# 256 KB copies of Wx into DRAM that nothing reads, issued from ScalarE's queue in the later steps of a recurrent layer

## The chip, the cores and the metric

The kernel runs on one core of a Trainium2 chip. The core has five engines with a queue of instructions each: TensorE (PE in the profile, its weight loads PEld), VectorE (DVE), ScalarE (ACT), GpSimd (POOL) and SyncE (SP), which issues transfers. Sixteen DMA engines move data between DRAM, where inputs and outputs lie, and the memory on the core. The metric is device time in microseconds (us) of one execution; lower is better.

## The reference

64 sequences of 256 steps with 1024 features pass through two layers, each added to its own input.

```python
# layer 0: x = x + rnn(x, h0 = cond)
xW = einsum('ntd,dh->nth', x, Wx) + b
def step(prev_h, xw):
    next_h = tanh(prev_h @ Wh + xw)
    return next_h, next_h
# layer 1: x = x + L1(x, q_pool = cond)
h = silu(q_pool @ W1.T + b1)
gate = sigmoid(h @ W2.T + b2)
# a Haar transform along time, every coefficient times gate, the inverse transform:
return v + a
```

Since every coefficient of the transform is multiplied by the same gate of its feature, the second layer comes down to a product: the output is (2 + gate) times the output of layer 0. The kernel keeps 2 + gate in the tile `factor`. All data are fp32.

## The kernel before

The recurrence is serial: step t needs the h of step t - 1. One step is the product of h (64 x 1024) with Wh (1024 x 1024), done by Strassen's scheme as seven products of half size (`strassen_product`, PE L199, 7 products of 16 fp32 matmuls of the program per step), with the sums between them on DVE and the copies out of PSUM and the tanh on ACT. The products x Wx do not depend on h. They are made for two steps at a time (128 rows, one "slab" of x) as three rounded partial products, 48 matmuls of 128x512 each (`x_matmul`, L278), to reach fp32 precision.

After twelve opening steps (`ALONE = 12`) the main loop, from step 12 on, works in groups of two steps. A group is: the x products of one coming slab (`beside_x`, "the x phase"), and then the h products of two steps ("the h phase"). The orders of PE, DVE, ACT, POOL and SP are written out by hand (`manual_schedule`): each engine runs its instructions in the order of the program text, and semaphores hold it where it needs the result of another.

The transfers of a group, all on SP's queue, in order: the finished sums of a slab go to DRAM (`store`, L390, 512 KB), a new slab of x is loaded (L121, 512 KB), the sums come back in the layout that a step needs (`reload`, L403, eight loads of 64 KB into `xw`), and a finished slab goes to the output (`store_y`, L634, 512 KB). The store of the sums has an added dependency (`not_ahead_of`) on `mark`, the copy of `u` in the group's second step, with the reason given in the code: "transfers stay out of the products of h". The relay, from that store until the `xw` of a step is back, must be done before `put_part` (L618) copies `xw` into the PSUM banks in which the step's products accumulate.

On ACT a step of the main loop is, in order: `y` (L778, the first product's copy out of PSUM), the cast of x for the coming slab (first step of a group only, L313), tanh of quarter 0 (L760), `put_part` for the next step's quarter 0 (first step only), `u` (L798), `put_part` 2 (first step only), tanh of quarters 3 and 2, tanh of quarter 1, `put_part` 1 (first step only). In the x phase ACT copies the two mixed sums out of PSUM (`take_mixed`, L323) and then does all three `put_part` of the next step. Each quarter of tanh is transposed by DVE (L764), and the transposed quarters and sums of them (`strassen_sides`, L229 to L232) are the weights of the next step's products. Their order there is: quarter 0, quarter 3, quarter 1, and then the sums.

Each DMA adds to one of eight completion semaphores, which are taken in turn over SP's and ACT's transfers together. A DMA is not issued before the semaphore's previous user has landed; where the issuing engine has not waited for that already, it waits at the DMA.

The first five slabs, which were finished before `factor` was known, are parked in DRAM and brought back step by step, one step in every second group (`kept_step`), all of it before step 80.

Of the kernel before, what the change touches and what calls it, by code (L numbers as in the profile page):

```python
# [53 lines left out]
F32 = mybir.dt.float32  # L54
# [6 lines left out]
N, T, D = 64, 256, 1024  # L61
P = 128
R = 32
Q = P // R
B = D // P
G = N // R
F = D // Q
W = G * F
# [3 lines left out]
M = 2  # L72
# [9 lines left out]
RINGS = 1024  # L82
BLOCK = 256
PLACE = 60


@with_exitstack
def tile_cond_resid(
# [14 lines left out]
    nc = tc.nc  # L103
# [7 lines left out]
    dram = ctx.enter_context(tc.tile_pool(name="dram", bufs=2, space=bass.MemoryType.DRAM))  # L111
# [82 lines left out]
    def strassen_product(out, a, i: int, first: bool = False) -> None:  # L194


        for k in range(KB):
            for q in range(Q):
                nc.tensor.matmul(  # L199
                    out=out[q * R : (q + 1) * R],  # L200
                    lhsT=a[:, k * R : (k + 1) * R],
                    rhs=wh_s.sides[i][k][:, q],
                    start=first and k == 0,
                    stop=k == KB - 1,
                    skip_group_check=True,
                    tile_position=(0, q * R),
                )
# [65 lines left out]
    def bank(tag: str, name: str):  # L273
        return one_pool.tile([P, HALF], F32, tag=tag, name=name)

    def x_matmul(acc, v, which: int, h: int, k: int, start=False, stop=False) -> None:

        nc.tensor.matmul(  # L278
            out=acc[h],
            lhsT=v[:, k * P : (k + 1) * P],  # L280
            rhs=wx_s[k][which][:, h * HALF : (h + 1) * HALF],
            start=start and k == 0,
            stop=stop and k == B - 1,
        )

    class XWork:
# [48 lines left out]
        def whole(self, aligned: bool = False) -> None:  # L335
# [8 lines left out]
            for h in range(2):  # L344
                for k in range(B):
                    if aligned and h == 1 and k == B - 2:
                        nc.tensor.addr_align(BLOCK, PLACE)
                    x_matmul(self.main, self.x0, 0, h, k, stop=True)
# [162 lines left out]
    kept, again, factor = [], [], None  # L511
# [103 lines left out]
    def put_part(t: int, j: int):  # L615

        part = bank(("acc", "m57", "gate")[j], f"acc{t}_{j}")[:, :E]
        nc.scalar.copy(part, xws[t // S][t % S][:, j])  # L618
        return part

    def residual(t: int, hT) -> None:
        v = x_step(t)
        nc.vector.tensor_add(v, v, blocks(hT))

    def not_ahead_of(dma, ins) -> None:
        tc.add_manual_dep(
            dma.ins,
            ins.ins.name,
            mybir.DependencyInfo(mybir.DependencyClass.Sync, mybir.DependencyReason.DATA),
            reason="transfers stay out of the products of h",  # L630
        )
# [26 lines left out]
    def beside_x(t: int, later, coming, scaled: list, end: int, mark):  # L658


        if later:
            d, dma = later.store()
            not_ahead_of(dma, mark)
        fresh = loaded[0] < NP
        load_next()
        if later:
            xws[later.i] = later.reload(d, True)
        now, half = coming, len(scaled) // 2
        many = now.i + 1 < NP and now.i <= end // S
        now.whole(not many)  # L670
        residual(t, hT)
        for r in scaled[: half + 1]:
            scale(pairs[r // S], r % S)
        if many:
            store_done(scaled[half])
            load_next()
        now.take_mixed()
        if mark:
            accs[:] = [put_part(t + 1, j) for j in range(3)]

        def prepare():
            if now.i + 1 == NP:
                return None
            nxt = XWork(now.i + 1)
            nxt.difference()
            nxt.low()
            return nxt

        nxt = prepare()
        if not fresh and not factors:  # L690

            x_n, factor_n = ends[0][:, :W], ends[0][:, W:]
            nc.vector.transpose(factor_n, factor)
            nc.vector.tensor_mul(x_n, x_n, factor_n)
            factors.append(factor_n)
        now.finish_half(0)
        now.finish_half(1)
        for r in scaled[half + 1 :]:
            scale(pairs[r // S], r % S)
        kept_step()  # L700
        if now.i <= end // S:
            d, _ = now.store()
            store_done(t)
            xws[now.i] = now.reload(d, True)
            if many:
                now = nxt
                now.cast()
                now.whole()
                now.take_mixed()
                nxt = prepare()  # L710
                now.finish_half(0)
                now.finish_half(1)
                return now, nxt
            return None, nxt
        store_done(t)
        return now, nxt

    again = []

    def kept_step() -> None:  # L720

# [25 lines left out]
    for t in range(ALONE, T):  # L747
        i, s = divmod(t, S)
        final = t == T - 1
        last_of_group = t == first + groups[0] - 1  # L750
        xw = xws[i][s]
        m16, m5, m7 = (bank(tag, f"{tag}_h{t}")[:, :E] for tag in ("m16", "main0", "main1"))
        y = sums.tile([P, 4, E], F32, tag="y", name=f"y{t}")
        u = sums.tile([P, E], F32, tag="u", name=f"u{t}")
        h = work.tile([P, W], F32, tag="h", bufs=1, name=f"h{t}")
        hT = None if final else work.tile([P, W], F32, tag="hT", name=f"hT{t}")
        nxt = [None] * 3

        def tanh(j: int) -> None:
            nc.scalar.activation(quad(h, j), quad(h, j), AF.Tanh)  # L760

        def transpose(j: int) -> None:
            if not final:
                nc.vector.transpose(quad(hT, j), quad(h, j))  # L764

        def put_next(j: int) -> None:
            if not last_of_group:
                nxt[j] = put_part(t + 1, j)

        def times_factor(v: slice) -> None:  # L770
            nc.vector.tensor_mul(h[:, v], h[:, v], ends[0][:, W + v.start : W + v.stop])

        def plus_x(v: slice) -> None:
            nc.vector.tensor_add(h[:, v], h[:, v], ends[0][:, v])
            nc.sync.dma_start(out=yT[i][:, W + v.start : W + v.stop], in_=h[:, v])

        strassen_product(m16, sides[1], 1, True)
        nc.scalar.copy(y[:, 0], m16)  # L778
        if t == first and coming is not None:
            coming.cast()  # L780
        strassen_product(accs[2], sides[4], 4)
        strassen_product(accs[0], sides[2], 2)
        strassen_product(m5, sides[5], 5, True)
        nc.vector.tensor_add(quad(h, 0), accs[0], y[:, 0])  # L784
        tanh(0)
        nc.vector.tensor_add(y[:, 3], m5, xw[:, 3])
        transpose(0)
        if final:
            times_factor(slice(0, E))
            plus_x(slice(0, E))  # L790
        elif t > T - 4:

            v = x_step(t - 1)
            nc.vector.tensor_mul(v, v, blocks(factor))
            store_y(i - 1) if t == T - S else None
        put_next(0)
        strassen_product(m16, sides[6], 6)
        mark = nc.scalar.copy(u, m16)  # L798
        nc.vector.tensor_add(y[:, 3], y[:, 3], u)
        nc.vector.tensor_add(y[:, 2], accs[2], u)  # L800
        put_next(2)
        strassen_product(m7, sides[7], 7, True)
        for o in (3, 2):
            nc.vector.tensor_add(quad(h, o), m7, y[:, o])
        tanh(3)
        tanh(2)
        nc.vector.tensor_add(y[:, 1], m5, u)
        transpose(3)
        strassen_product(accs[1], sides[3], 3)
        nc.vector.tensor_add(quad(h, 1), accs[1], y[:, 1])  # L810
        tanh(1)
        if final:
            times_factor(slice(F, W))
            times_factor(slice(E, F))
            plus_x(slice(E, F))
            plus_x(slice(F, W))
            break
        transpose(2)
        put_next(1)
        transpose(1)  # L820
        sides = strassen_sides(hT, t)
        accs = nxt
        if t == T - 2:

            last = slab("last")
            residual(t, hT)
            nc.vector.tensor_mul(blocks(last[:, :W]), x_step(t), blocks(factor))
            nc.sync.dma_start(out=yT[i][:, :W], in_=last[:, :W])
        elif last_of_group:
            group = range(first, t + 1)  # L830
            first = t + 1
            del groups[0]
            later, coming = beside_x(t, later, coming, list(group), t + groups[0], mark)
        else:
            residual(t, hT)
# [34 lines left out]
```

## Time and profile before

| what | value |
|---|---|
| median of 3 runs | 3045.01 us (3044.51 to 3046.28) |
| the profiled execution | 3044.8 us, of which the span from first to last instruction is 3043.0 us |
| granted TensorE clock | 1.000 |
| PE / PEld / DVE / ACT / POOL busy | 3033.8 / 2706.8 / 1797.0 / 871.0 / 844.4 us |
| time that DMA packets took, share of 16 engines' span | 27.5% (transfers), 1.1% (queue 8, instructions) |
| HBM read and written | 154.93 MB and 136.31 MB |
| one group of two steps | 23.47 us |

The group's length is read from the timeline: the x phases of two groups begin at 1143.87 and 1167.34 us. "Idle before" in the profile is time of the engine ahead of an instruction, with what ended it; "issue" is idle time in which the engine waited for nothing that the profile shows. Packets' shares are of the time of all 16 DMA engines. A view with a window cuts the window into 40 equal slices, each digit being the busy share in tenths.

### The profile page before, as it was taken

To read this page: it belongs to the slowest core of one execution; us is meant where nothing else is said; L and a number is where in the kernel's file an instruction comes from. 1 tells how busy PE (TensorE), PEld (TensorE's weight loads), DVE (VectorE), ACT (ScalarE), POOL (GpSimd) and SP (SyncE) were. 2 spreads that over 40 slices of the span, in tenths; PEclk is the share of its full clock that TensorE was granted. 3 is DMA by queue.
4 is the path that set the end of the run, shared out by engine and by line. 5 is a ranking of instruction groups with operands and counts; after the bars stand their busy time and mean duration, and the time that the engine had idled before them with its cause. 6 is when DMAs were issued, how large, how long until landed. Compare 5 with 4: busy or idle time off the path is not lost.

```text
span 3043.0 us, 144709 instructions
## 1 busy us (share of the span) xinstructions
PE 3033.8 (100%) x63862; PEld 2706.8 (89%) x63862; DVE 1797.0 (59%) x4928; ACT 871.0 (29%) x2641; POOL 844.4 (28%) x521
## 2 busy tenths in 40 slices
PE   9999999999999999999999999999999999999999
PEld 6888899889988898889888998899889988998888
DVE  8556555655555555555555565555655565565555
ACT  3222222222222222222222322232222222222222
POOL 2233333332223222322232223222222222222321
PEclk9999999999999999999999999999999999999999
DMA  7323323332222222222222222222222222222222
GB/s 264 123 90 115 101 100 100 109 107 86 86 101 98 86 86 99 100 86 86 96 99 89 86 93 97 95 86 89 102 95 86 86 102 97 86 86 102 97 86 76
DMA packets 164616, 300.59 MB, mean 99 GB/s; under 512 B 44192, under 2 KB 110496, under 8 KB 164000
## 3 DMA queue, kind: packets, MB, share of 16 engines
q1 hardware_dynamic: 163856, 290.81, 27.5%
q8 instruction: 514, 8.42, 1.1%
q14 instruction: 102, 0.84, 0.1%
q10 hardware_dynamic: 144, 0.52, 0.0%
HBM read 154.93 MB, written 136.31 MB: 96 GB/s over the span
## 4 chain that ended last, share of the span: by engine, by line
PE 98%; DMA 1%; POOL 0%; issue 0%; DVE 0%; SPq 0%; DVEq 0%; ACT 0%
PE main L278 30%; PE acc L199 22%; PE mixed L278 16%; PE m_h L199 15%; PE main_h L199 14%; PE m L199 1%; DMA h0T<-condT 0%; DMA wh<-wh 0%; DMA w<-w1T 0%; POOL sum L324 0%; PE gate_ps L216 0%; DMA x<-xT 0%; DMA b_row<-b 0%; DVE x L302 0%; SPq L134 0%
## 5 line engine op out<-in xcount | busy, mean ns | idle before, releaser
L278 PE MATMUL main<-wx,x 128*128 128x512 f32 x4064 | 945.7, 389 | 0.3 <-DVE x L302 0.3
L505 POOL TENSOR_TENSOR x<-x,factor 128x512 f32<-128x512 f32 x242 | 358.4, 1481 | 2030.8 <-issue 1177.2
L278 PEld LDWEIGHTS main<-wx,x 128*128 128x128 f32 x4064 | 762.0, 188 | 161.2 <-issue 2.2
L278 PE MATMUL mixed<-wx,x 128*128 128x512 f32 x2032 | 499.1, 397 | 0.0
L324 POOL TENSOR_TENSOR sum<-sum,b_row 128x512 f32<-128x512 f32 x254 | 448.1, 1784 | 50.6 <-DMA w<-w1T 43.2
L278 PEld LDWEIGHTS mixed<-wx,x 128*128 128x128 f32 x2032 | 371.7, 188 | 97.9 <-issue 24.8
L760 ACT ACTIVATE h<-h 128x128 f32<-128x128 f32 x976 | 275.7, 306 | 547.8 <-DVE h L784 330.9
L302 DVE TENSOR_TENSOR x<-x,x_high 128x1024 fp32r<-128x1024 f32 x127 | 171.1, 1347 | 253.6 <-PE main L278 253.5
L764 DVE STREAM_TRANSPOSE hT<-h 128x128 f32<-128x128 f32 x972 | 298.0, 307 | 38.2 <-ACT h L760 38.1
L380 DVE SCALAR_TENSOR_TENSOR sum<-main,sum 128x512 f32<-128x512 f32 x254 | 175.6, 691 | 206.2 <-PE main L278 204.5
L199 PE MATMUL acc<-wh,s 128*32 128x128 f32 x8160 | 270.8, 273 | 1.2 <-issue 1.2
L199 PE MATMUL acc<-t,hT 128*32 128x128 f32 x8160 | 270.9, 273 | 0.7 <-issue 0.7
L199 PE MATMUL acc<-wh,hT 128*32 128x128 f32 x8160 | 269.9, 273 | 0.0
L778 ACT COPY y<-m_h 128x128 f32<-128x128 f32 x244 | 65.0, 267 | 709.7 <-PE m_h L199 694.6
L199 PE MATMUL m_h<-wh,hT 128*32 128x128 f32 x7808 | 261.4, 274 | 0.3 <-issue 0.3
L199 PE MATMUL main_h<-t,s 128*32 128x128 f32 x7808 | 259.6, 273 | 0.0
L199 PE MATMUL m_h<-t,s 128*32 128x128 f32 x7808 | 258.8, 273 | 0.1
L199 PE MATMUL main_h<-wh,s 128*32 128x128 f32 x7808 | 258.6, 273 | 0.0
L199 PEld LDWEIGHTS m_h<-wh,hT 128*32 128x32 f32 x7808 | 208.6, 110 | 44.7 <-issue 44.7
L618 ACT COPY acc<-xw 128x128 f32<-128x128 f32 x732 | 177.8, 264 | 234.3 <-DMA xw<-sum_d 165.0
L323 ACT ACTIVATE sum<-mixed 128x512 f32<-128x512 f32 x254 | 152.0, 599 | 320.9 <-PE mixed L278 320.8
L307 DVE SCALAR_TENSOR_TENSOR x<-x_high,x 128x1024 fp32r<-128x1024 f32 x127 | 190.7, 1502 | 86.9 <-PE mixed L278 86.8
(81 smaller groups left out, 2931.7 us busy)
## 6 DMA issues: line engine op xcount, KB each, us to landing
x<-xT SPq DMA_DIRECT2D x127, 512.0 KB, 4.0
sum_d<-sum SPq DMA_DIRECT2D x127, 512.0 KB, 2.9
xw<-sum_d SPq DMA_DIRECT2D x1016, 64.0 KB, 2.0
yT<-x SPq DMA_DIRECT2D x122, 512.0 KB, 2.7
wh<-wh SPq DMA_DIRECT2D x8, 512.0 KB, 10.9
w<-w1T SPq DMA_DIRECT2D x8, 512.0 KB, 8.5
w<-w2T SPq DMA_DIRECT2D x8, 512.0 KB, 4.0
wx<-wx SPq DMA_DIRECT2D x7, 512.0 KB, 8.5
```

What stands on the lines that cost most here:

```text
L199: nc.tensor.matmul(out=out[q * R : (q + 1) * R], lhsT=a[:, k * R : (k + 1) * R], rhs=wh_s.sides[i][k][:, q], start=first and k == 0, stop= ...
L278: nc.tensor.matmul(out=acc[h], lhsT=v[:, k * P : (k + 1) * P], rhs=wx_s[k][which][:, h * HALF : (h + 1) * HALF], start=start and k == 0, s ...
L302: nc.vector.tensor_sub(self.x1, x, self.high)
L307: nc.vector.scalar_tensor_tensor(out=self.x2, in0=self.high, scalar=1.0 + DOWN, in1=pairs[i], op0=ALU.mult, op1=ALU.subtract)
L323: nc.scalar.activation(s, self.mixed[h], AF.Copy, scale=-1.0)
L324: nc.gpsimd.tensor_add(s, s, b_row[:, h * HALF : (h + 1) * HALF])
L380: nc.vector.scalar_tensor_tensor(out=v, in0=self.main[h], scalar=1.0 + DOWN, in1=v, op0=ALU.mult, op1=ALU.add)
L505: nc.gpsimd.tensor_mul(of_step(x, s), of_step(x, s), blocks(factor))
L618: nc.scalar.copy(part, xws[t // S][t % S][:, j])
L760: nc.scalar.activation(quad(h, j), quad(h, j), AF.Tanh)
L764: nc.vector.transpose(quad(hT, j), quad(h, j))
L778: nc.scalar.copy(y[:, 0], m16)
```

## The change

A function `flow` issues, from ACT's queue, a DMA of 128 rows of 2 KB, 256 KB in all, from one of the eight blocks of Wx in DRAM to a tile in DRAM (eight such tiles in turn). No instruction reads these tiles. The function does nothing before the step that its argument names, nor in the last two steps. The calls with `LOW` act from step 80: five in each step (behind `y`, tanh 0, `u`, tanh 2 and tanh 1) and one in the x phase, 11 per group. The calls with `LIFT` act from step 160: two in each step (behind the places of `put_part` 0 and 2) and one in the x phase. With these a group of the built program has 16 such DMAs, where the description of the change in words says 14: the even steps have 7, and the odd ones, with the x phase behind them, 9. In all there are 1190. The orders of PE, DVE, POOL and SP stay as they were; semaphores are taken in turn over more DMAs, so which one a transfer uses, and which earlier transfer it waits for, shifts.

```diff
+LOW = 80
+LIFT = 160
@@ in beside_x
         now.take_mixed()
+        flow(LOW)
         if mark:
             accs[:] = [put_part(t + 1, j) for j in range(3)]
+            flow(LIFT)
@@
-    again = []
+    again, flows = [], [0]
+
+    def flow(least: int) -> None:
+
+        if t < least or t + M >= T:
+            return
+        n = flows[0]
+        flows[0] += 1
+        v = dram.tile([P, W], F32, tag="flow", bufs=8, name=f"flow{n}")
+        nc.scalar.dma_start(out=v, in_=wx[n % B][:, :W])
@@ in the loop over steps
         strassen_product(m16, sides[1], 1, True)
         nc.scalar.copy(y[:, 0], m16)
+        flow(LOW)
...
         tanh(0)
+        flow(LOW)
         nc.vector.tensor_add(y[:, 3], m5, xw[:, 3])
...
         put_next(0)
+        flow(LIFT)
         strassen_product(m16, sides[6], 6)
         mark = nc.scalar.copy(u, m16)
+        flow(LOW)
         nc.vector.tensor_add(y[:, 3], y[:, 3], u)
         nc.vector.tensor_add(y[:, 2], accs[2], u)
         put_next(2)
+        flow(LIFT)
         strassen_product(m7, sides[7], 7, True)
...
         tanh(3)
         tanh(2)
+        flow(LOW)
...
         tanh(1)
+        flow(LOW)
         if final:
```

## The prediction

> **What bounds the kernel now.** I read the page first: its busy table, its chain, then one steady group (1143.9 to 1167.3 us) in the transfer view and in the timelines of ACT, SP and PE, and last the final group.
>
> ```profile
> span 3043.0 us, 144709 instructions
> PE 3033.8 (100%) x63862; PEld 2706.8 (89%) x63862; DVE 1797.0 (59%) x4928; ACT 871.0 (29%) x2641; POOL 844.4 (28%) x521
> ...
> PE 98%; DMA 1%; POOL 0%; issue 0%; DVE 0%; SPq 0%; DVEq 0%; ACT 0%
> ```
>
> The chain that ended last is 98% PE. Nothing that ACT or the DMA engines do now sets the end, so the change can't take away a wait of any size; it can only leave PE alone or make it wait. The steady groups all take 23.47 us.
>
> The transfers of one group, in 40 slices of 0.585 us:
>
> ```profile
> DMA  9889540254359930000000010000001000002007
> GB/s 399 238 315 420 168 121 11 61 133 144 119 172 375 413 154 0 0 0 0 0 0 0 0 28 0 0 0 0 0 0 28 0 0 0 0 0 56 0 0 322
> ...
> q1 hardware_dynamic: 1065, 2.07, 25.0%
> q8 instruction: 4, 0.07, 1.0%
> ```
>
> Everything on SP's queue passes in the x phase (the first fifteen slices and the last). In the h phase the 16 DMA engines stand still but for isolated slices of 28 GB/s, which are packets of queue 8: 16 KB of instructions each, four per group. The change fills exactly this empty stretch. Two slices are full: 420 GB/s at nine tenths busy is the best rate this trace shows.
>
> ACT in the first h step of that group, where a late ACT hurts (behind the second step comes the x phase of some 11 us, in which PE needs nothing of h):
>
> ```profile
> 1158.26 0.31 ACT L760 ACTIVATE h<-h 128x128 f32<-128x128 f32 x1 [0.88 <-DVE h L784]
> 1158.48 0.26 ACT L618 COPY acc<-xw 128x128 f32<-128x128 f32 x1
> 1159.62 0.27 ACT L798 COPY u<-m_h 128x128 f32<-128x128 f32 x1 [0.88 <-PE m_h L199]
> 1160.44 0.27 ACT L618 COPY acc<-xw 128x128 f32<-128x128 f32 x1 [0.56 <-DVE y L800]
> 1160.81 0.51 ACT L760 ACTIVATE h<-h 128x128 f32<-128x128 f32 x2
> 1161.69 0.31 ACT L760 ACTIVATE h<-h 128x128 f32<-128x128 f32 x1 [0.36 <-DVE h L810]
> ```
>
> ACT idles before nearly every one of these, and the new DMAs go into the idle stretches. What an issue costs is seen on SP's queue, and how soon PE needs the last tanh on PE:
>
> ```profile
> 1166.02 0.34 SPq L390 DMA_DIRECT2D sum_d<-sum  x1
> 1166.41 0.43 SPq L121 DMA_DIRECT2D x<-xT  x1
> ```
>
> ```profile
> 1162.86 1.06 PE L199 MATMUL acc<-wh,hT 128*32 128x128 f32 x32
> ```
>
> The product at 1162.86 is the first that reads quarter 1 of the next h. Its tanh ends at 1162.00, the transpose behind it takes 307 ns (its group's mean): 0.5 us of slack.
>
> **The sum's base.** Everything is added to the profiled execution, 3044.8 us (span 3043.0 and 1.8 around it); the median of the runs, 3045.01, is 0.2 above it. Resolution: 0.2% is 6 us, about what this kernel's measurement can tell from no change.
>
> **The change, part by part.** Nothing is removed, and PE, DVE, POOL and SP keep their orders. Added are DMAs of 256 KB: 11 per group in steps 80 to 159 (40 groups) and, by the calls in the built program, 16 (not 14) in steps 160 to 253 (47 groups).
>
> *Issue time on ACT.* A DMA of 128 rows costs its queue 0.34 to 0.43 us (rows above). With 11 per group the step's gaps take them: 0.88 us ahead of `u` holds one issue, 0.56 behind it one, and 0.36 ahead of the last tanh one, at most 0.07 late. With 16 there are two in the 1.05 us between tanh 0 and `u`, beside a copy of 0.26 (0.94 to 1.12: up to 0.07 late), two between `u` and tanh 3 in 0.93 us with a copy of 0.27 (up to 0.20 late), and the last at most 0.07: 0.34 us in all at the dearer issue, under the slack of 0.5. Cost taken: nothing, hidden by PE's products that stand between; low end also nothing. If an issue on ACT took 0.55 us, the same sum gives 0.94 us late, 0.4 over the slack, in one step of 47 groups: +20 us, the high end.
>
> *The wait for a semaphore.* Some flows wait for the flow issued six to eight DMAs before, or for a store of y from the group before. Behind a waiting flow stand the tanh and `put_part` on ACT, behind these DVE's transposes and then PE. As long as a flow lands within some 5 us this costs nothing, since six flows are issued over about 5 us; it costs as soon as flows pile up. SP's transfers take turns with them: the reloads of `xw` now wait for the last flows of the h phase to land. The relay has room: the copies of `xw` run at 1149.9, and PE's first product that needs one starts at 1155.9, 6 us later.
>
> *DMA engine time.* This decides. No transfer of this trace goes from DRAM to DRAM, so the price is bounded. Low end: a flow costs what a load of its size does at the best slice, 0.262 MB / 420 GB/s = 0.62 us of all 16 engines. With the group's own 2.16 MB (5.1 us) that makes 12.0 us at 11 flows and 15.1 at 16, of 23.47: no cost. High end: it crosses DRAM twice and pays both crossings at the group's mean price (26.3% of 23.4 us, the queues' shares with queue 14, are 6.15 us for 2.16 MB, so 2.85 us per MB): 1.49 us. 11 flows and the rest then take 22.6 us, just inside the group; 16 take 30.0, or 6.6 us too many in 47 groups: +308. I take two crossings at the best rate, because a load has DRAM on one side and a store on the other, both are rows here, and a flow is one of each: 1.25 us. 11 flows: 13.7 + 5.1 = 18.9 us, 80% of the group, which fits. 16 flows: 20.0 + 5.1 = 25.1 us, 1.65 us more than the group lasts. The engines then set the pace; flows pile up, ACT waits at their semaphores, tanh comes late, and PE waits for hT. 47 x 1.65 = +77 us.
>
> *Instruction packets.* They share the engines with the flows of the h phase. In steady groups PE waits for "issue" only at the change of phase (0.35 us) and now and then for 0.17. But in the last group, with its h steps in a row and no x phase between them, it shows what a supply at its limit looks like:
>
> ```profile
> 3017.44 0.27 PE L199 MATMUL acc<-wh,s 128*32 128x128 f32 x1 [1.18 <-issue]
> ...
> 3025.39 0.30 PE L199 MATMUL m_h<-wh,hT 128*32 128x128 f32 x2 [0.29 <-issue]
> ...
> 3033.16 0.30 PE L199 MATMUL acc<-t,hT 128*32 128x128 f32 x2 [0.32 <-issue]
> ```
>
> So the margin in an h phase is small. Low end 0 (a packet slips between others). High end: 0.3 us for each of three packets of an h phase, 87 groups: +78. I take 0, as the slices of full load at the group's start hold a packet too and no wait follows; but there PE eats instructions slowly, so this is a rival below.
>
> Here the Trainium skill speaks otherwise: "Runtime: NRT & Kernel Launch", section "Instruction fetch mechanics", says that an engine's queue fetches the next 16 KiB block while the current one runs, and that crossing a block's border is mostly hidden. By it this term is 0 whatever the load; by the rows of the last group it is not hidden when PE runs h products without pause. The rows decide that the risk is kept.
>
> Sum: 3044.8 + 0 (issue) + 77 (engines, steps 160 on) + 0 (packets) = 3122 us.
>
> **Rivals.** *Not slower: flows are cheap.* If a flow costs the DMA engines up to 1.14 us ((23.47 - 5.1)/16), the 16 fit and all else is hidden: 3045 us. For it: ACT's gaps, the empty slices, PE's chain. Against: two crossings at the best rate are 1.25, so some overlap must help. The point that decides is that 1.14.
>
> *Instruction packets come late in both stages.* Three per h phase by 0.3 us: +78 in 87 groups, 3123; by 0.1 us +26, 3071. For it: the waits of the last group. It shows from step 80 on, unlike my forecast.
>
> *The high price.* At 1.49 us per flow, 3353; halfway from 1.25, 3237. For it: the mean price has queueing in it, and the flows queue; against: the full slices.
>
> *ACT's issue.* 0.55 us each: 3065.
>
> *Faster.* The occasional waits of 0.17 for issue go away, if traffic keeps transfers quick: some groups last 23.6 to 23.7 instead of 23.47, not 2 us in the whole span. So 3043, inside the resolution. More than 0.2% faster would need a wait that the chain does not have.
>
> **How the numbers follow.** Chances: the forecast (steps from 160 held by the DMA engines, 3060 to 3200) 0.33; not slower 0.31; packets late in both stages 0.18; the high price 0.11; ACT's issue 0.04; faster by over 0.2% 0.03. Slower is 0.33 + 0.18 + 0.11 + 0.04 = 0.66, the same 0.31. Range: its low end, 3043, takes in the case of no change; the high end, 3250, leaves out about half of the high price and the worst mixtures of late packets and piled flows, some 0.14, and faster below it, 0.03. The forecast's own range is 3060 to 3200.
>
> **What would show it.** Right: groups of steps 80 to 159 stay at 23.47 us; those from 160 last about 25 us, their DMA slices are full throughout, ACT's flows wait on DMA, and PE idles behind DVE's or ACT's h. Wrong: groups at 23.47 to the end (flows cheap); groups longer from step 80 on with PE idle on issue (packets); DMA slices half empty and yet PE waiting for tanh (issue time on ACT).

## The result and the profile after

| what | before | after |
|---|---|---|
| median of four runs | 3045.65 us (3044.51 to 3046.34) | 3211.76 us (3204.46 to 3214.12) |
| ratio, after to before | | 1.0542 (95% interval 1.0523 to 1.056) |
| the profiled execution | 3044.8 us | 3213.23 us (span 3211.4) |
| granted TensorE clock | 1.000 | 0.996 |
| one group, steps before 80 | 23.48 us | 23.48 us |
| one group, steps 80 to 159 (11 copies) | 23.48 us | 24.74 us |
| one group, steps from 160 (16 copies) | 23.48 us | 25.96 us |

The change costs 166 us, 5.4%. The last three rows are means over the groups' x phases in the trace, from the start of one to the start of the next. They account for the whole loss: 40 groups by 1.25 us are 50, 47 groups by 2.48 us are 117, together 167. The prediction had 0 and 77 in the same places.

The page of the profile after; the first lines are the span and each engine's busy time, then the DMA share in 40 slices of the span, the queues (q10 is ACT's, which carries the copies, q1 is SP's), the chain that ended last, and one group of PE's instructions with its idle time behind the last bar:

```profile
span 3211.4 us, 145897 instructions
PE 3089.3 (96%) x63862; PEld 2717.3 (85%) x63862; DVE 1847.1 (58%) x4928; ACT 884.7 (28%) x2641; POOL 838.7 (26%) x521
...
DMA  6332333322235666666666666888778777777786
...
q10 hardware_dynamic: 171504, 312.55, 33.0%
q1 hardware_dynamic: 163856, 290.81, 26.4%
...
PE 94%; issue 4%; DMA 2%; POOL 0%; DVE 0%; ACT 0%; ACTq 0%; SPq 0%; DVEq 0%
...
L201 PE MATMUL main_h<-t,s 128*32 128x128 f32 x7808 | 284.2, 273 | 102.4 <-issue 102.2
```

Two things are to be seen. The chain was 98% PE and had 0% of issue; now issue has 4% of it. And the DMA engines are not full: six tenths in the slices of steps 80 to 159, seven to eight tenths later. Windows in the steps before 80, from 80 and from 160 say it closer; the columns are window, length, busy us (instructions) of PE, PEld, DVE, ACT and POOL, granted clock, DMA share and GB/s:

```profile
509.70:955.70 446.00, 446.00 (x9428) 400.94 (x9424) 261.63 (x742) 128.09 (x400) 129.15 (x79) 1.00 0.29 97
1003.10:1894.50 891.40, 862.13 (x17859) 760.88 (x17856) 509.87 (x1405) 248.38 (x757) 229.09 (x144) 1.00 0.65 204
2018.80:3058.30 1039.50, 969.78 (x19844) 850.54 (x19840) 582.24 (x1561) 275.42 (x841) 255.13 (x160) 0.99 0.79 245
```

The share goes from 0.29 to 0.65 and 0.79, and PE, which was busy throughout, stands for 29 of 891 us and then for 70 of 1040. A copy cost 0.89 us of all sixteen engines (33.0% of 3211.4 us over 1190 copies), well under the 1.25 of the forecast.

What PE waited for over the whole span; the columns are what was waited for, us in total, times, and the longest:

```profile
PE main_h L201 <- issue: 102.2, 78, 2.5
PE acc L201 <- issue: 7.8, 24, 1.0
PE m_h L201 <- issue: 4.1, 2, 2.8
...
PE acc L201 <- DVE hT L777: 1.0, 2, 0.7
```

Before, the waits of PE for issue came to 2.2 us:

```profile
PE acc L199 <- issue: 1.9, 4, 1.2
...
PE m_h L199 <- issue: 0.3, 1, 0.3
```

The wait for the transposed h (`hT`), which was to carry the forecast's loss, is 1.0 us in all. The two waits of `m_h` (1.27 and 2.79 us) are in the last group, where the kernel before waited 0.29 and 0.32. These sums fall short of the 167 us, because the profile models the ends of matmuls: a product held up in its middle appears as a longer product plus a shorter idle time. One group at 11 copies shows it (start, duration, engine, line, tile):

```profile
1515.43 1.45 PE L201 MATMUL acc<-wh,s 128*32 128x128 f32 x32
1516.74 1.08 PE L201 MATMUL m_h<-wh,hT 128*32 128x128 f32 x32
...
1519.36 1.08 PE L201 MATMUL main_h<-t,s 128*32 128x128 f32 x31
1521.02 0.30 PE L201 MATMUL main_h<-t,s 128*32 128x128 f32 x1 [0.57 <-issue]
1521.14 1.08 PE L201 MATMUL m_h<-t,s 128*32 128x128 f32 x32
```

Normally one product starts 0.87 us after another. The product `main_h<-t,s` runs 31 of its 32 matmuls, stops, and runs the last one late; its successor starts 1.78 us after it, 0.91 too late, of which the profile calls 0.57 idle. The product at 1515.43 lasts 1.31 to its successor, 0.44 too long, and no idle time is named at all. So I measure from start to start. The mean lengths (us) of the 14 h products of a group, where those not listed are 0.87 to 0.93:

```
                       7th    8th    11th   12th   13th   14th
before                 0.87   0.87   0.89   0.87   0.87   0.99
after, steps 80-159    1.12   0.87   1.86   0.87   0.87   0.99
after, from step 160   1.10   0.92   2.81   0.93   0.96   1.05
```

The loss sits at two places of the group: in the last product of the first step and in the fourth of the second. They are four products apart. A product is 32 matmul and 32 weight-load records, so four products are 256 instructions. That is about what a packet of queue 8 holds: the queue carried 514 packets of 16 KB, and PE's 63862 matmuls and as many weight loads make 248 for each of them.

The transfers of the same kind of group, in 40 slices of 0.62 us, at 11 copies:

```profile
DMA  7899998999693104459901851386676687739615
...
q10 hardware_dynamic: 1616, 2.94, 42.4%
q1 hardware_dynamic: 1072, 2.10, 24.0%
q8 instruction: 4, 0.07, 1.0%
```

The stretch that was empty before is now filled, in parts to nine tenths. A packet of instructions takes as long as it did once it has begun (mean 1.06 us before, 1.04 at 11 copies, 0.98 at 16). It begins later. In the kernel before, each packet of the h phase begins soon after PE has passed a border: the second one at 6.2 to 7.3 us from the start of the h phase, the border behind the 7th product being at 6.1. At 11 copies it begins at 7.15 to 9.45 us, at 16 at 8.5 to 10.6. And PE goes on a fixed time after it has landed: in all 85 groups from step 80 on in which the 11th product took more than 1.0 us, the 12th starts 1.05 to 1.63 us behind the landing, with a median of 1.5. So at 0.87 us a product a packet that lands later than about 8.1 us from the start of the h phase makes PE stand (the border that it serves is at 9.6). In the kernel before 17 of 120 groups had such a landing, 8.34 us at the latest, and ten of these lasted 23.53 to 23.70 us instead of 23.47.

### The profile page after: what moved, and what is told of

Read it like the earlier page. It is cut to its first block, busy times and chain, and to the rows that moved or that the text cites. A ratio compares the mean times of both kernels' runs of the same rounds, so it can differ in the third digit from the quotient of the medians.

```text
span 3211.4 us, 145897 instructions
## 1 busy us (share of the span) xinstructions
PE 3089.3 (96%) x63862; PEld 2717.3 (85%) x63862; DVE 1847.1 (58%) x4928; ACT 884.7 (28%) x2641; POOL 838.7 (26%) x521
## 3 DMA queue, kind: packets, MB, share of 16 engines
q10 hardware_dynamic: 171504, 312.55, 33.0%
## 4 chain that ended last, share of the span: by engine, by line
PE 94%; issue 4%; DMA 2%; POOL 0%; DVE 0%; ACT 0%; ACTq 0%; SPq 0%; DVEq 0%
PE main L280 29%; PE acc L201 21%; PE mixed L280 15%; PE main_h L201 14%; PE m_h L201 14%; PE m L201 1%; DMA h0T<-condT 0%; DMA wh<-wh 0%; DMA w<-w1T 0%; PE gate_ps L218 0%; POOL sum L326 0%; DMA x<-xT 0%; DMA xw<-sum_d 0%; DMA b_row<-b 0%; DMA sum_d<-sum 0%
## 5 line engine op out<-in xcount | busy, mean ns | idle before, releaser
L201 PE MATMUL main_h<-t,s 128*32 128x128 f32 x7808 | 284.2, 273 | 102.4 <-issue 102.2
L201 PEld LDWEIGHTS main_h<-t,s 128*32 128x32 f32 x7808 | 228.4, 110 | 125.1 <-issue 125.0
L304 DVE TENSOR_TENSOR x<-x,x_high 128x1024 fp32r<-128x1024 f32 x127 | 197.8, 1558 | 219.3 <-PE main L280 219.3
L201 PE MATMUL acc<-wh,s 128*32 128x128 f32 x8160 | 286.1, 274 | 8.1 <-issue 7.6
L201 PE MATMUL main_h<-wh,s 128*32 128x128 f32 x7808 | 266.4, 276 | 0.0
L309 DVE SCALAR_TENSOR_TENSOR x<-x_high,x 128x1024 fp32r<-128x1024 f32 x127 | 218.5, 1721 | 60.1 <-PE mixed L280 57.4
L325 ACT ACTIVATE sum<-mixed 128x512 f32<-128x512 f32 x254 | 145.1, 598 | 330.3 <-DMA sum_d<-sum 208.6
```

The costliest lines, as they stand in the source:

```text
L201: nc.tensor.matmul(out=out[q * R : (q + 1) * R], lhsT=a[:, k * R : (k + 1) * R], rhs=wh_s.sides[i][k][:, q], start=first and k == 0, stop= ...
L304: nc.vector.tensor_sub(self.x1, x, self.high)
L309: nc.vector.scalar_tensor_tensor(out=self.x2, in0=self.high, scalar=1.0 + DOWN, in1=pairs[i], op0=ALU.mult, op1=ALU.subtract)
L325: nc.scalar.activation(s, self.mixed[h], AF.Copy, scale=-1.0)
```

## The experiments

The theory after this reading: a packet of instructions queues behind packets of copies in a DMA engine, lands after PE has run out, and PE stands at the border of its block of 256. The rivals: ACT's queue (its issues, and the semaphores that the added DMAs share), and saturated DMA engines that delay the relay of `xw` or the tanh. All experiments edit the changed kernel. A result is one execution with its profile, beside one execution of the kernel before on the same chip; differences are to that one. Group lengths and product lengths are read from the traces as above.

**Only the first stage's copies.** The eleven `LOW` copies go on to the end, the `LIFT` copies are gone.

```diff
-LIFT = 160
+LIFT = T
```

> Steps 80 to 253 with 11 copies of 256 KB per group, the five more from step 160 left out. In the changed kernel the 40 groups with 11 copies last 24.8 us on the mean instead of 23.47, with PE idle on issue in the h phase. Theory A (PE's instruction packets come late behind the copies): the 47 later groups cost the same 1.3 us each, so +113 us, 3158 us, and all of it as issue time. Theory B (my forecast: the DMA engines' total time sets the pace from step 160): 11 copies fit, so +52 us at most, the part already seen, and nothing from step 160 on. The granted clock, 0.996 in the changed kernel with seven short halvings after 2300 us, is 1.000 if it is the five more copies that lower it.

Measured: 3149.96 us against 3048.79, +101. A group takes 24.59 us in steps 80 to 159 and 24.70 from 160 on; the 7th product takes 1.12 and 1.11 us, the 11th 1.71 and 1.85. Where PE waited:

```profile
PE main_h L201 <- issue: 52.8, 67, 1.7
```

So eleven copies cost 1.1 to 1.25 us per group in either stage, and from step 160 the five further copies are responsible for the rest of the 2.48. The stage itself, or the place in the program, is not the cause.

**The same issues with few bytes.** Every copy keeps its place, its queue and its semaphore, but carries 256 bytes per row, 32 KB in all.

```diff
-        v = dram.tile([P, W], F32, tag="flow", bufs=8, name=f"flow{n}")
-        nc.scalar.dma_start(out=v, in_=wx[n % B][:, :W])
+        v = dram.tile([P, 64], F32, tag="flow", bufs=8, name=f"flow{n}")
+        nc.scalar.dma_start(out=v, in_=wx[n % B][:, :64])
```

> All 1190 copies stay where they are on ScalarE, with their 128 rows and their semaphore waits, but a row is 256 bytes instead of 2 KB: 32 KB each, an eighth of the bytes. Theory A (instruction packets wait behind the copies' bytes): nearly all of the +167 us goes, at most +20 remain. Theory C (issue time and semaphore waits on ScalarE make tanh late): the issues are all still there, so +100 us or more remain, with PE idle behind VectorE's h or hT and not on issue.

Measured: 3049.15 us against 3048.79; groups of 23.52 and 23.55 us. The queue's line on the page and PE's waits:

```profile
q10 hardware_dynamic: 171504, 39.59, 5.9%
```

```profile
PE main_h L201 <- issue: 1.1, 5, 0.3
```

The 171504 packets are all there, and the wait is gone. 1190 issues on ACT and the order of the semaphores cost nothing that could be measured; what costs is the time that the copies occupy the DMA engines. Small copies also land early, so this run alone does not exclude waits at semaphores for copies that land late; that PE waited on issue, and not behind what ACT delivers, speaks against them.

**Half the bytes, over eight engines and over sixteen.** Both copy 64 rows, 128 KB. The rows are arranged so that the outer dimension is 8 in one (below) and 16 in the other, which has `a=16` in both places. The Trainium skill, "DMA: Bandwidth & Descriptors", section "Why a DMA increments its semaphore by 16 and not by 1", states that the outer dimension decides over how many engines a transfer goes, by the largest number up to 16 that divides it, and that from these queues they are the lowest-numbered ones. The traces agree with the number: beside its packets of data each copy has packets of 4 bytes, 16 of them in the changed kernel and 8, 12 and 15 in the runs meant to use 8, 12 and 15 engines. Which engine a packet took is not in the trace, so no run here shows that part.

```diff
-        v = dram.tile([P, W], F32, tag="flow", bufs=8, name=f"flow{n}")
-        nc.scalar.dma_start(out=v, in_=wx[n % B][:, :W])
+        v = dram.tile([P // 2, W], F32, tag="flow", bufs=8, name=f"flow{n}")
+        nc.scalar.dma_start(
+            out=v[:].rearrange("(b a) f -> a b f", a=8),
+            in_=wx[n % B][: P // 2, :W].rearrange("(b a) f -> a b f", a=8),
+        )
```

Eight:

> All 1190 copies in place, but 128 KB each, as 8 rows of 8 pieces of 2 KB, so that a copy should use only 8 of the 16 DMA engines, each with the same eight packets as in the changed kernel; the other 8 engines are free of copies. Theory A, if what matters is the queue of the engine that brings instructions: either all of the loss stays (instructions come by one of the 8 used engines; +150 us) or all of it goes (by one of the others; under +15 us). If it is DRAM or the path as a whole, half of the bytes leave about half of the loss, +50 to +100 us.

Sixteen:

> The same 128 KB copies over all 16 engines, four packets of 2 KB on each: the partner of the run with 8 engines. Theory A by bytes: +40 to +90 us. If only the number of copies mattered: +167 us. If only an overload of the engines mattered (theory B): 0.

Measured, sixteen: 3069.74 us, +21; groups of 23.61 and 23.87 us, the 11th product at 0.99 and 1.19. Half the bytes cost a tenth of the time in steps 80 to 159 (0.13 us per group instead of 1.25) and a sixth from 160 (0.39 instead of 2.48). The cost is no price per byte; it begins where a packet's delay passes what it has to spare.

Measured, eight: 3205.0 us, +156. That is the total expected if all of the loss stays, but by another cause. Steps 80 to 159 lost far less than half of 1.25 us and behaved like half the bytes over sixteen engines, 23.70 us a group with the 11th product at 1.05, though each engine that carries copies carried as many packets as in the changed kernel. From step 160 on a group takes 26.66 us, and the loss has another cause, as PE's waits say:

```profile
PE main_h L201 <- DVE sum L382: 87.7, 45, 3.3
PE acc L201 <- DVE hT L780: 17.3, 30, 0.8
...
PE main_h L201 <- issue: 1.4, 6, 0.3
```

PE now stands at the third h product (2.98 us instead of 0.87) behind a sum on DVE and at other products behind `hT`, and hardly ever on issue. ACT and DVE in that stage (2018.8 to 3136.8 us):

```profile
DVE hT L780 <- ACT h L776: 351.9, 194, 6.1
...
ACT h L776 <- DMA xw<-sum_d: 191.7, 42, 6.3
...
ACT h L776 <- DMA flow<-wx: 173.8, 42, 6.0
```

ACT's tanh stands behind late reloads and late copies, DVE behind the tanh, and PE behind DVE. This is the mechanism of the forecast: copies that pile up delay what ACT and the relay must deliver. It exists, but in a kernel that gives the whole load to fewer engines.

**Fifteen engines, and sixteen with the same bytes.** If a packet of instructions waits in the queue of one particular engine, a transfer that leaves one engine out may or may not hit it. 120 rows go to 15 engines by the rule named above; the second kernel copies the same 240 KB with 128 rows of 1920 bytes, `[P, 480]` from `wx[n % B][:, :480]`.

```diff
-        v = dram.tile([P, W], F32, tag="flow", bufs=8, name=f"flow{n}")
-        nc.scalar.dma_start(out=v, in_=wx[n % B][:, :W])
+        v = dram.tile([120, W], F32, tag="flow", bufs=8, name=f"flow{n}")
+        nc.scalar.dma_start(out=v, in_=wx[n % B][:120, :W])
```

Fifteen:

> All 1190 copies in place with 120 rows of 2 KB instead of 128: 15 rows' groups of eight, so that a copy uses 15 of the 16 DMA engines with eight packets on each, 94% of the changed kernel's bytes. Theory A1 (instruction packets wait in the queue of one engine, and it is the one left out): the waits on issue at the two places of the h phase (7th product of the first step, 4th of the second, 0.25 and 0.97 us per group in steps 80 to 159) go, and the groups of that stage last under 23.7 us. Theory A2 (it is another of the upper eight engines, or the load on DRAM as a whole): the waits stay, 24.6 to 24.8 us per group, about +150 us in all.

Sixteen:

> The partner of the run with 15 engines: the same 240 KB per copy in the same places, but as 128 rows of 1920 bytes, so over all 16 engines. If the one engine left out made the difference: 24.5 to 24.7 us per group in steps 80 to 159 (against 23.91 with 15 engines and 24.74 with 256 KB), and about +145 us in all. If the few bytes less did: 23.9 us, and +85 us.

Measured: fifteen 3129.67 us against 3045.07, +85; sixteen 3189.59 against 3047.94, +142. In steps 80 to 159 a group takes 23.91 and 24.53 us, so with equal bytes the loss over 23.48 is 0.43 and 1.05; the 11th product takes 1.23 and 1.68. From 160 on the groups are 24.90 and 25.60 us. The kernel with 15 thus met neither expectation, under 23.7 us or 24.6 to 24.8: most of the loss went, but not all. PE's waits, of the kernel with 15 first:

```profile
PE main_h L201 <- issue: 23.3, 34, 1.7
PE acc L201 <- DVE hT L777: 16.6, 41, 0.8
```

```profile
PE main_h L201 <- issue: 89.9, 76, 2.7
```

The bytes are the same, and each engine that is used carries as many packets in both (8 per copy, slightly larger ones where there are 15), and yet three fifths of the loss go in steps 80 to 159 when one engine is spared. The second packet begins at 7.4 us from the start of the h phase with 15 engines and at 8.05 with 16 (means; 6.65 before). That fits instruction packets that wait mostly in one engine's queue, and one that is left out here. It is argued, not shown, since the trace has no engine numbers. In steps from 160 a new wait comes up, behind `hT` (the 8th product at 1.38 us instead of 0.87): with the border's wait shortened, the forecast's late tanh is next in line.

**Twelve engines**, 192 KB with as many packets on each used engine as in the changed kernel:

```diff
-        v = dram.tile([P, W], F32, tag="flow", bufs=8, name=f"flow{n}")
-        nc.scalar.dma_start(out=v, in_=wx[n % B][:, :W])
+        v = dram.tile([96, W], F32, tag="flow", bufs=8, name=f"flow{n}")
+        nc.scalar.dma_start(
+            out=v[:].rearrange("(b a) f -> a b f", a=12),
+            in_=wx[n % B][:96, :W].rearrange("(b a) f -> a b f", a=12),
+        )
```

> The same with 12 engines, eight packets of 2 KB on each (192 KB). If instructions come by one of the last four engines: groups of steps 80 to 159 under 23.7 us, with the load on the used engines as in the changed kernel. If by one of engines 9 to 12, or if the load on DRAM decides: 24.2 us and more. From step 160 on the relay of the sums may be late as in the run with 8 engines (26.7 us per group), by waits on DMA and not on issue.

Measured: 3262.9 us against 3045.07, +218. Steps 80 to 159 take 23.74 us a group, just over the 23.7 expected if one of the last four engines brings instructions, with the 11th product at 1.09, as with eight engines (23.70, 1.05). From 160 on 27.87, with the third product at 3.52 and the waits of the eight-engine kernel:

```profile
PE main_h L201 <- DVE sum L382: 113.0, 45, 3.3
...
PE main_h L201 <- issue: 7.2, 15, 1.3
```

Between 15 and 12 engines the first stage improves little (0.43 to 0.26 over 23.48) though another fifth of the bytes is gone too, between 12 and 8 hardly at all (0.22), so the larger part hangs on the step from 16 to 15. What remains at 12 and 8 engines, some 0.2 us per group, are late packets too: the second packet begins at 7.2 and 7.1 us there, and in the groups of steps 80 to 159 with a long 11th product (16 and 19 of 40) PE goes on 1.3 to 1.6 us behind its landing. Why it still begins later than before, beside copies that should spare its engine, is open.

**Six copies, in the x phase or in the h phase.** All other copies are removed. In the first kernel six stand together in the x phase; in the second, three of the calls with `LOW` are kept in each h step, those behind `u`, tanh 2 and tanh 1.

```diff
         if mark:
             accs[:] = [put_part(t + 1, j) for j in range(3)]
+        for _ in range(6):
+            flow(LOW)
```

> Six copies of 256 KB per group from step 80 on, all behind the three put_part of the x phase, none in the h phase. Theory A: the first block of instructions of a group has some 8 us to spare there, so the copies cost nothing unless they run on into the h phase: 23.47 to 23.6 us per group, under +12 us in 87 groups. Theory B' (the relay of the sums is delayed by the copies and PE waits for xw): +0.5 us or more per group, +40 us and more, with PE behind ScalarE's acc.

```diff
         tanh(0)
-        flow(LOW)
...
         mark = nc.scalar.copy(u, m16)
         flow(LOW)
...
         put_next(2)
-        flow(LIFT)
...
         tanh(2)
         flow(LOW)
...
         tanh(1)
         flow(LOW)
```

> The same six copies of 256 KB per group from step 80 on, three in each h step (behind u, tanh 2 and tanh 1), none in the x phase. Theory A: between the half-size copies (+0.13 us per group) and the eleven (+1.26): +0.2 to +0.8 us, +20 to +70 us in all, at the two places of the h phase where a block of instructions ends. If only the bytes per group count and not their place: the same as the six in the x phase.

Measured: 3062.49 us for the x phase (+17; groups of 23.66 and 23.70 us) and 3052.56 for the h phase (+7.5; 23.55 and 23.59). Both expectations were missed, under +12 for the x phase and +20 to +70 for the h phase, and in opposite directions. In the x phase, where PE eats its instructions slowly, they cost more than spread among the h products. The mean products show where: at six in x the 7th 0.94 and the 11th 0.97, at six in h only the 11th, 0.94. I had taken the phase for what matters. With six in a row the first packet of the h phase begins later (3.35 us on the mean in steps 80 to 159, against 2.86 with six spread and before); that these copies keep the engines busy into the h phase fits this, but is argued. Six copies spread cost 0.07 us per group in that stage and eleven 1.25: the first ones fall within what a packet has to spare.

**Another place of the border.** The program has a constant that sets where in a block of 256 instructions the main loop of PE begins. Moved by 128, the borders of blocks must move by two products.

```diff
-PLACE = 60
+PLACE = 188
```

> The changed kernel with the place of PE's program within its blocks of 256 instructions shifted by half a block (PLACE 188 instead of 60). An h product has 64 instructions, so the ends of blocks move from the 3rd, 7th and 11th of the fourteen products of a group to the 1st, 5th, 9th and 13th. Theory A (PE waits for a block to arrive): the waits move with them, from the 7th and 11th product to the 5th and 9th, and perhaps the 13th; steps before 80 may last a little longer too. If the waits belong to certain products (their operands, or the copies issued at that moment): they stay at the 7th and 11th. The total is expected between 3150 and 3300 us.

Measured: 3309.09 us against 3047.94, +261. The waits moved by two products: the 9th and the 13th take 1.21 and 2.46 us in steps 80 to 159 and 1.68 and 2.95 from 160, while the 7th and the 11th are back to normal. (The expectation had the 5th and 9th, the 13th only perhaps, and 3300 us at most.) The same group as above, in PE's timeline:

```profile
1501.47 1.05 PE L201 MATMUL main_h<-wh,s 128*32 128x128 f32 x30
1503.92 0.38 PE L201 MATMUL main_h<-wh,s 128*32 128x128 f32 x2 [1.40 <-issue]
```

The product that stands is another one, of other tiles (`main_h<-wh,s`, the 13th), and PE's waits for issue over the span are longer than in the changed kernel (102.2 and 7.8):

```profile
PE main_h L201 <- issue: 137.5, 89, 3.3
PE acc L201 <- issue: 37.8, 68, 1.9
```

Nothing else in the program moved, neither the copies nor the order of any engine. A wait that moves with the border of 256 instructions and not with the tiles belongs to the instructions. The other borders, at the 1st and 5th product, show next to no wait (0.90 and 0.87 us in steps 80 to 159, 0.91 at the 5th from 160). The packet for the 1st has the x phase in which to arrive, as the one for the 3rd product of the changed kernel has; the packet for the 5th begins only 0.5 us behind the border before it (mean of steps 80 to 159), those for the 9th and 13th 1.5 and 2.7 us behind theirs. Here too PE goes on 1.2 to 1.6 us after the landing in every group from step 80 on with a long 9th or 13th product. The dearer place also has a price without copies: before step 80 a group takes 23.73 us with it, its first one left aside, against 23.48.

**How late the packet begins, in all runs.** The last border of the h phase decides most of the loss. The table has, as means of a stage, how long after the start of the 8th product (PE has then passed the border ahead) the second packet begins, and the length of the 11th product, at the end of which the packet is needed:

```
                                       begins after   11th product
before, steps 80-159                      0.51           0.89
few bytes, steps 80-159                   0.75           0.91
six copies in the x phase, 80-159         0.91           0.97
half the bytes, 16 engines, 80-159        0.92           0.99
eight engines, 80-159                     0.94           1.05
six copies in the h phase, 80-159         0.95           0.94
twelve engines, 80-159                    1.01           1.09
fifteen engines, 80-159                   1.21           1.23
sixteen engines, 240 KB, 80-159           1.68           1.68
after, steps 80-159                       1.74           1.86
after, from step 160                      2.98           2.81
```

Add the 1.04 us of the packet and the 1.5 us until PE goes on to 1.74, and take off the 3.5 us of four products: 0.8 us late at 11 copies, where 0.97 was lost; in the same way 2.0 at 16 copies, where 1.94 was lost. So the delay ahead of the packet's start accounts for the loss at the 11th product.

## Why the prediction was wrong

Forecast 3122 us, measured 3211.76: the sign was right and the size less than half of what came (77 of 166 us). The sign came by luck: the term that gave the 77 cost nothing, and the term taken as 0 gave the 166. Its steps in order:

**Issue time on ACT: 0.** Right in its cost: with the same 1190 issues and few bytes the kernel took 3049.15 us against 3048.79. The price of 0.34 to 0.43 us read on SP's queue was too low, though; on ACT an issue took 0.50 us (median of the 1190), near the 0.55 of the high end, and it stayed hidden:

```profile
1511.39 0.50 ACTq L731 DMA_DIRECT2D flow<-wx  x1
```

**The wait for a semaphore: 0 at 11, the cost of piled-up copies at 16.** Right for the end, and the signs came in part. ACT does wait for copies from step 160, and the relay is later than before (the copies of `xw` waited at most 1.9 us for it in a like stretch of the kernel before). These are ACT's waits in that stretch after, from 2018.8 to 3136.8 us, in the columns of PE's waits above:

```profile
ACT acc L620 <- DMA xw<-sum_d: 141.9, 32, 5.7
...
ACT u L814 <- DMA flow<-wx: 48.6, 15, 4.8
ACT acc L620 <- DMA flow<-wx: 48.1, 11, 6.2
```

PE lost next to nothing by them (1.0 us behind `hT` in the span). It stood at its own borders meanwhile. In the run with 15 engines, where those waits are shorter, it waited 16.6 us behind `hT`.

**DMA engine time: 1.25 us a copy, +77, "This decides".** This step failed. A copy took 0.89 us of the engines, under the 1.14 that I had named as the point from which 16 fit, and the engines were 65% busy from step 80 and 79% from step 160. By this term alone the kernel would have been as fast as before (16 copies and the group's own 5.1 us make 19.4 of 23.47). The reasoning asked when the engines are full; the loss begins long before. (In the transfer view four slices, not two, are at nine tenths, with 375 to 420 GB/s; the price hardly changes by it.)

**Instruction packets: "I take 0", high end 0.3 us for each of three, +78.** This is the step that decided, and its size was wrong on both ends: not three borders per group but two, at 0.25 and 0.99 us with 11 copies and 0.23 and 1.94 us with 16, the last over six times the high end. The 0.3 came from two of the three rows of the last group; the third row, printed beside them, has 1.18 us, and the high end left it out without a reason. The 0 was argued from the start of the groups, where the engines are full and a packet passes without a wait. There PE is in the x phase, though, and has time. In the h phase PE eats 256 instructions in four products, 3.5 us. In the kernel before, the second packet landed at 7.1 to 8.3 us, on the mean 7.8, and was needed at about 8.1: at most 1.0 us to spare, in some groups none. The copies made it begin 1.5 us later on the mean at 11 (8.1 instead of 6.65 us) and 2.7 at 16. The rows of the last group were the right ones to read; the waits there were those of a supply without copies, and no upper bound for one with them.

**The Trainium skill's rule**, "Runtime: NRT & Kernel Launch", section "Instruction fetch mechanics", that crossing a block's border is mostly hidden, would have given 3045. The traces agree before the copies (2.2 us of issue waits in 3043.0) and contradict it under them (4% of the chain). The measurement decides.

**The rivals.** "Instruction packets come late in both stages" was the right mechanism, with its sign as told (groups longer from step 80, PE idle on issue), held at 0.18 and priced at 3123. "Flows are cheap" was right on the engines' time (0.89 us) and wrong on the conclusion. The high price, 1.49 us a copy, did not come.

**Signs named.** "Groups of steps 80 to 159 stay at 23.47" and "DMA slices full throughout" fell; "groups longer from step 80 on with PE idle on issue" came. That groups from step 160 last "about 25 us" came near (25.96), but by the borders and not by the DMA engines' time.

What is shown: the time is lost at the borders of PE's blocks of 256 instructions (their places, and their moving by two products), the cause is the occupation of the DMA engines by copies (the same issues with few bytes cost nothing), and packets begin later while taking no longer, with PE going on a fixed time after they land. What is argued: that most of the delay arises in the queue of one engine, the one that 120 rows leave out. What is open: why the packets still begin later beside copies on eight or twelve engines, at about 0.2 us per group in steps 80 to 159.

## What to carry to other kernels

The engine's own instructions arrive by DMA. Where an engine runs 256 instructions in a few microseconds (here 3.5 us), a block may have a microsecond or less to spare, and bulk transfers beside it can eat that while the DMA engines' mean share looks harmless (65% here). Look for idle on "issue" at places that lie 256 instructions apart, measure from start to start since part of the wait is drawn into the product before, and keep what must run beside such a stretch few, short and spread: six copies cost 0.07 us per group when spread, 0.19 in a row, and eleven 1.25.

## What the runs showed of the hardware that was not expected

The waits also cost clock. In the changed kernel seven stretches of 3.413 us each ran at half the clock, by the records of the granted clock, all of them after step 160; the kernel before had none. PE's timeline around the first one:

```profile
2320.16 1.08 PE L201 MATMUL main_h<-t,s 128*32 128x128 f32 x31
2323.18 0.33 PE L201 MATMUL main_h<-t,s 128*32 128x128 f32 x1 [1.95 <-issue]
2323.31 1.94 PE L201 MATMUL m_h<-t,s 128*32 128x128 f32 x32
2324.98 1.93 PE L201 MATMUL main_h<-wh,s 128*32 128x128 f32 x32
2326.69 1.09 PE L201 MATMUL acc<-wh,s 128*32 128x128 f32 x32
```

The two products behind the pause take 1.94 and 1.93 us where they take 1.08. Each stretch costs about 1.7 us, the six in the groups from step 160 some 10 of the 117 us of that stage (the seventh is in the last group). Each followed a pause of PE of about 2.2 to 3.1 us, counted from the start of one matmul to that of the next (here 2.22 us from 2320.96 on), but not every such pause was followed by one (2.42 and 2.48 us at 2090 and 2502 us were not). With the eleven copies alone no pause inside the loop was longer than 1.94 us, and no stretch of half clock came. The kernels with eight engines, twelve engines and the moved border had 16, 21 and 14 of them.

The stretches begin at whole multiples of 3.4133 us from one another (69, 130, 153, 184, 237 and 256 of them after the first). If the time is cut into intervals on that grid, each of the seven follows an interval in which PE stood for 2.17 to 3.07 us; of all other intervals one has 2.21 us and the rest at most 2.11. The pauses at 2090 and 2502 us lie across the border of two intervals, with at most 1.4 and 1.5 us in one. So in this kernel it is the part of a pause that falls into one interval that decides, at about 2.2 us. In the kernels with eight engines, twelve engines and the moved border the two sides overlap between 1.9 and 2.3 us.

The Trainium skill, "TensorE: Matmul & The Clock Gate", section "Part 1: The HAM clock gate (the "warmup" mystery)", tells of a window of about 3.4 us after which an idle TensorE falls to half its clock. The length of 3.413 us agrees with it; that a pause of 2.2 us can suffice is shorter than that window.
